# Tracing layer 0's products with values two key blocks behind their exponentials, for images 1 to 3

## The chip, the cores and the metric

The kernel runs on one core of one Trainium2 chip. The metric is the device time of one execution in microseconds; three executions before the change gave 4298.08, 4301.13 and 4314.65, median 4301.13. All arithmetic is in 32-bit floating point.

## The reference, cut to what matters

The input is a batch of 4 images of 32 x 32 positions with 384 channels. Four layers follow one another, each added to its input: deformable attention (layer 0), attention with a group weight (layer 1), a ratio of box sums (layer 2) and an outlook attention (layer 3). The change touches the attention of layer 0 alone:

```python
attn = jnp.einsum('bmhc,bnhc->bhmn', qh, k) * scale
...
bias = _bilinear_sample(rpe_img, disp)
bias = bias.reshape(Bq, G, n, n, GH).transpose(0, 1, 4, 2, 3).reshape(Bq, HEADS, n, n)
attn = jax.nn.softmax(attn + bias, axis=-1)
out = jnp.einsum('bhmn,bnhc->bmhc', attn, v).reshape(Bq, Hq, Wq, NC)
```

There are 6 heads of 64 channels and n = 1024 positions. Each head has 1024 x 1024 scores, and the bias is sampled bilinearly from a table at positions that depend on the key.

## The kernel before, in words

**Two lanes.** `Trunk` computes layers 1 to 3 of an image, `Front` computes layer 0. Image 0's layer 0 runs first, by itself and by a method of its own (`heads0`), which keeps a written-out order. After that, layer 0 of image b + 1 runs beside layers 1 to 3 of image b. Both lanes are Python generators that trace instructions. Each hands over by yielding a weight: a trunk image has weights that add up to 1109, a front image 714. `layer3` of the class `Net` (the driver) runs the trunk to its next yield, and then the front as long as it is less than a tenth of an image ahead. So weights decide only in which order the two lanes' instructions are traced. A half block of the trunk's attention (half of one key block j of a head pair in `pair`) has weight 7, which lets the front go on by about 4.5 of its units.

**From trace to queues.** The framework plans the order on each engine's queue from the trace: it steps through a model of the program and gives a free engine the ready instruction that was traced first. It also gives out buffers then. So the traced order is a priority, not the order of execution. Only `keep_in_program_order` and `issue_after` fix an order; the lines of `head0`, which the change touches, use neither. On the chip each engine works through its queue in order.

**A half head.** `head0(h, q)` does head h for half of the queries (q is 0 or 1, 512 queries). The 1024 keys are 8 blocks of 128 keys (NJ = 8); each block's scores are one tile `lg` of 128 keys x 512 queries. There are 12 half heads an image and 36 in the three images.

- For each key block a gather brings a window of the bias table (L955), ScalarE and VectorE interpolate it (L967 to L973), TensorE computes the products of keys and queries (L979), and VectorE adds (L982) and keeps a running maximum `rmax` (L984, L986). After every second block the front yields 6.
- The maximum over all keys is taken by transposes (L993), a reduction (L997) and a product that spreads it over the partitions (L1001). ScalarE copies it to `tb` (L1005). The front yields 3.
- For each key block VectorE subtracts `tb` (L1012), ScalarE takes the exponential in place (L1013), and TensorE adds the product with the values into one bank `po` (L1014). The values carry a column of ones, so `po` also holds the sum of the exponentials. After every second block the front yields 2.
- ScalarE copies the result out of `po` into `queries` (L1018) and the row of sums over the tile of the first block (L1027, in `sums_of`). SP issues the DMA of the sums to memory (L1020). The front yields 3.

After both halves of two heads, `over_sums` loads the sums back (L1283), inverts them and multiplies.

**Buffers.** The score tiles `lg` rotate through 13 buffers, of which a half head holds 8. The windows have 4. Accumulators of one bank come from `bank()`, with 4 buffers for both lanes: `po`, the scores' products (two at a time), the trunk's sums over keys `av` (L1690, held for a whole head pair), and the trunk's products of similarities (L1748) and transposes (L1743). Accumulators of two banks come from `big()`, with 2 buffers: the trunk's scores (L1718) and first pass (L1580).

**The trunk beside it.** For each key block of a head pair, `pair` traces scores (L1718), their exponentials (L1726) and four products (L1743, L1748). Each product's bank is read by VectorE (L1755) and, for some, copied by ScalarE (L1760). After the first two or three products it queues a step of the first pass for the next pair (L1580 on TensorE, L1589 on VectorE, L1593 on ScalarE).

Of the kernel before, what the change touches and what calls it, by code (L numbers as in the profile page):

```python
# [20 lines left out]
AF = mybir.ActivationFunctionType  # L21
ALU = mybir.AluOpType
# [8 lines left out]
NJ = N // P  # L31
# [35 lines left out]
def bc(ap, axis, n):  # L67

    u = ap.unsqueeze(axis)
    shape = list(u.shape)  # L70
    shape[axis] = n
    return u.broadcast_to(shape)
# [368 lines left out]
class Front(Lane):  # L441
# [500 lines left out]
    def head0(self, h, q):  # L942

        nc, v = self.nc, self.nc.vector
        f = self.f
        k, r0 = h // 2, (h % 2) * GC
        rows = slice(r0, r0 + GC)
        HH, HN = HW // 2, N // 2
        queries = self.qpad[rows, k, 1 + HH * q : 1 + HH * (q + 1), 1 : 1 + HW]
        logits = []  # L950
        rmax = self.wt([P, HN], "rmax", 2)
        for j in range(NJ):
            c = j * G + h
            win = self.wt([P, (HH + 1) * WROW], "win", 4)
            nc.gpsimd.indirect_dma_start(  # L955
                out=win,
                out_offset=None,
                in_=self.strips[:, :],
                in_offset=bass.IndirectOffsetOnAxis(
                    ap=self.widx[:, q, c : c + 1], axis=0  # L960
                ),
            )
            wv = win.rearrange("p (r c) -> p r c", c=WROW)
            sc = lambda i, t: f[:, i, t, c : c + 1]

            z = self.wt([P, HH, HW + 1], "z", 3)
            nc.scalar.activation(z, wv[:, 0:HH, 0 : HW + 1], AF.Copy, scale=sc(1, 1))  # L967
            v.scalar_tensor_tensor(  # L968
                z, wv[:, 1 : HH + 1, 0 : HW + 1], sc(0, 1), z, ALU.mult, ALU.add
            )  # L970
            lg = self.wt([P, HH, HW], "lg", 13)
            nc.scalar.activation(lg, z[:, :, 0:HW], AF.Copy, scale=sc(1, 0))  # L972
            v.scalar_tensor_tensor(lg, z[:, :, 1 : HW + 1], sc(0, 0), lg, ALU.mult, ALU.add)  # L973
            logits.append(lg.rearrange("p y x -> p (y x)"))
            if j % 2:
                ps = [self.bank() for _ in range(2)]
                for u in range(2):
                    w, mov = self.logits_of(h, q, j - 1 + u)
                    nc.tensor.matmul(ps[u], w, mov, start=True, stop=True)  # L979
                for u in range(2):  # L980
                    lf = logits[j - 1 + u]
                    v.tensor_tensor(lf, ps[u], lf, ALU.add)  # L982
                    if j - 1 + u == 1:
                        v.tensor_tensor(rmax, logits[0], lf, ALU.max)  # L984
                    elif j > 1:
                        v.tensor_tensor(rmax, rmax, lf, ALU.max)  # L986
                yield 6


        NI = HN // P  # L990
        ps = self.bank()
        for i in range(NI):
            nc.tensor.transpose(  # L993
                ps[:, i * P : (i + 1) * P], rmax[:, i * P : (i + 1) * P], self.ident
            )
        top = self.wt([P, NI], "top", 2)
        v.tensor_reduce(top, ps.rearrange("p (i n) -> p i n", i=NI), AX.X, ALU.max)  # L997
        diag = self.wt([P, NI, P], "diag", 1)
        v.tensor_tensor(diag, bc(self.ident, 1, NI), bc(top, 2, P), ALU.mult)
        ps = self.bank()  # L1000
        nc.tensor.matmul(  # L1001
            ps, self.ones, diag.rearrange("p i n -> p (i n)"), start=True, stop=True
        )
        tb = self.wt([P, HN], "tb", 2)
        nc.scalar.copy(tb, ps)  # L1005
        yield 3


        po = self.bank()
        for j in range(NJ):  # L1010
            lf = logits[j]
            v.tensor_tensor(lf, lf, tb, ALU.subtract)  # L1012
            nc.scalar.activation(lf, lf, AF.Exp)  # L1013
            nc.tensor.matmul(po, self.values_of(h, j), lf, start=j == 0, stop=j == NJ - 1)  # L1014
            if j % 2:
                yield 2

        nc.scalar.copy(queries, po[rows, :].rearrange("p (y x) -> p y x", y=HH))  # L1018
        den = self.sums_of(h, po, logits[0])
        nc.sync.dma_start(self.den[h][:, q * HN : (q + 1) * HN], den)  # L1020
        yield 3

    def sums_of(self, h, po, to):

# [1168 lines left out]
```

## Time and profile before

| | |
|---|---|
| median of three executions | 4301.13 us |
| the profiled execution | 4273.34 us |
| its span, first to last instruction | 4271.6 us |
| mean granted TensorE clock | 0.956 |
| TensorE busy | 3908.3 us, 91% |
| VectorE busy | 3109.2 us, 73% |
| ScalarE busy | 2300.2 us, 54% |
| GpSimd busy | 952.5 us, 22% |
| product with values (L1014), 576 instructions | 271.1 us busy, 17.2 us idle before |
| exponential (L1013), 288 instructions | 166.8 us busy, 29.5 us idle before |
| copy of the result (L1018), 36 instructions | waits 25.4 us for L1014, 11 times |

PE is TensorE, PEld its weight loads, DVE VectorE, ACT ScalarE, POOL GpSimd, SP the engine that issues most DMAs; a q after a name is the engine's sequencer. L1014 is line 1014 of the kernel before. A row such as "PE bank L1014 <- ACT lg L1013" tells that TensorE's instruction of L1014, which writes a tile named bank, waited for ScalarE's of L1013. One 32-bit product of 128 x 128 with 128 x 512 shows as two TensorE instructions. The profile's times come from one execution, which was 27.8 us shorter than the median.

### The profile page before, as it was taken

Reading aid. Unit: us, or ns where it says so; the run is one execution under the profiler, and the core shown is the slowest. Engines: PE = TensorE matmul, PEld = TensorE weight load, DVE = VectorE, ACT = ScalarE, POOL = GpSimd, SP = SyncE. Lnnn points to the kernel's source line nnn. Section 1 sums busy time; section 2 is a strip of 40 time slices with the busy share of each in tenths; the row PEclk is TensorE's granted clock in tenths of the full one; section 3 lists DMA queues with packets and bytes.
Section 4 is the critical chain, followed back from the end, with each engine's and each line's share of the span. In section 5 each row is a group of like instructions: output and inputs, shape, how many; then the busy total and the mean of one; then the engine's idle time right before and its main releaser. Section 6 shows DMA issues by size and latency. Waiting matters only on the chain.

```text
span 4271.6 us, 45276 instructions
## 1 busy us (share of the span) xinstructions
PE 3908.3 (91%) x14832; PEld 1680.1 (39%) x14832; DVE 3109.2 (73%) x5940; ACT 2300.2 (54%) x3640; POOL 952.5 (22%) x945
## 2 busy tenths in 40 slices
PE   8799989999999898999899989999999989999997
PEld 4333434333334443433333443433333434434443
DVE  4699676879888456787879837588888874566654
ACT  3277345667664333566767424376666542566633
POOL 1766152202121015221303002321121210000001
PEclk9899989999999998999999999999999999999998
DMA  7744353212221444321312163432221213210111
GB/s 162 227 133 124 88 162 100 72 43 83 61 82 41 143 137 145 104 71 47 96 39 84 33 195 123 137 97 61 60 84 51 79 63 120 86 39 23 34 34 45
DMA packets 295398, 385.09 MB, mean 90 GB/s; under 512 B 167858, under 2 KB 228798, under 8 KB 294650
## 3 DMA queue, kind: packets, MB, share of 16 engines
q1 hardware_dynamic: 246336, 217.44, 18.3%
q0 software_dynamic: 39936, 145.53, 11.6%
q10 hardware_dynamic: 8890, 19.23, 1.4%
q8 instruction: 118, 1.93, 0.2%
q14 instruction: 118, 0.97, 0.1%
HBM read 295.63 MB, written 86.75 MB: 90 GB/s over the span
## 4 chain that ended last, share of the span: by engine, by line
PE 52%; DVE 25%; ACT 8%; issue 6%; DMA 5%; POOL 3%; SPq 0%; DVEq 0%; ACTq 0%; POOLq 0%
PE bank L1748 12%; PE big L1718 6%; DVE nmax L1589 4%; PE big L418 4%; PE bank L1014 4%; PE big L1580 3%; PE bank L432 3%; DVE e L1755 3%; ACT big L1593 3%; PE bank L1690 3%; PE bank L1743 2%; PE bank L979 2%; POOL gat L762 2%; DVE lg L982 2%; PE big L678 2%
## 5 line engine op out<-in xcount | busy, mean ns | idle before, releaser
L1748 PE MATMUL bank<-whole,sg 128*128 128x512 f32 (+3 forms) x2304 | 844.8, 497 | 6.8 <-POOL sg L1701 5.3
L1755 DVE SCALAR_TENSOR_TENSOR e<-bank,gam,e 128x512 f32<-128x512 f32 x768 | 560.0, 746 | 273.5 <-PE bank L1748 179.9
L1593 ACT ACTIVATE big<-big,nmax 128x1024 f32<-128x1024 f32 x384 | 417.6, 1088 | 319.9 <-DVE nmax L1589 319.2
L1748 PEld LDWEIGHTS bank<-whole,sg 128*128 128x128 f32 x2304 | 397.0, 194 | 350.6 <-issue 258.1
L1589 DVE TENSOR_REDUCE nmax<-big 128x1 f32<-128x1024 f32 x384 | 451.9, 1217 | 57.3 <-PE big L1580 56.8
L955 POOL DMA_INDIRECT win<-strips,widx x288 | 310.9, 1080 | 781.2 <-DVE z L968 382.1
L1726 ACT ACTIVATE e<-big 128x1024 f32<-128x1024 f32 x384 | 380.2, 1020 | 188.1 <-PE big L1718 181.8
L1718 PE MATMUL big<-qa,ka 64*128 64x512 f32 x1536 | 423.4, 646 | 37.3 <-ACT big L1593 26.3
L1701 POOL TENSOR_SCALAR sg<-whole,gam 128x512 f32<-128x512 f32 x192 | 150.5, 784 | 1326.9 <-PE bank L1748 1009.0
L1580 PE MATMUL big<-k,q 32*128 32x512 f32 x1536 | 272.9, 670 | 51.7 <-ACT big L1593 30.2
L1014 PE MATMUL bank<-lg,va 128*128 128x512 f32 x576 | 271.1, 607 | 17.2 <-ACT lg L1013 17.1
L762 POOL DMA_INDIRECT gat<-pairs,sidx x192 | 220.3, 1148 | 293.1 <-DVE ix_one L561 235.8
L1718 PEld LDWEIGHTS big<-qa,ka 64*128 64x128 f32 x1536 | 145.7, 194 | 282.7 <-issue 110.8
L973 DVE SCALAR_TENSOR_TENSOR lg<-z,bias_f,lg 128x512 f32<-128x512 f32 x288 | 214.8, 762 | 36.6 <-ACT lg L972 35.3
L967 ACT ACTIVATE z<-win,bias_f 128x528 f32<-128x528 f32 x288 | 206.1, 736 | 52.9 <-DVE lg L973 31.9
L968 DVE SCALAR_TENSOR_TENSOR z<-win,bias_f,z 128x528 f32<-128x528 f32 x288 | 217.8, 767 | 21.8 <-ACT z L967 20.6
L1690 PE MATMUL bank<-e,vs 128*32 128x512 f32 x1536 | 221.5, 629 | 13.0 <-DVE vs L1684 13.0
L1012 DVE TENSOR_TENSOR lg<-lg,tb 128x512 f32<-128x512 f32 x288 | 184.1, 693 | 54.6 <-ACT tb L1005 54.6
L1760 ACT COPY gn<-bank 128x128 f32<-128x128 f32 (+2 forms) x288 | 106.3, 369 | 200.3 <-DVE e L1755 198.5
L972 ACT ACTIVATE lg<-z,bias_f 128x512 f32<-128x512 f32 x288 | 200.1, 716 | 10.0 <-DVE z L968 6.9
L982 DVE TENSOR_TENSOR lg<-bank,lg 128x512 f32<-128x512 f32 x288 | 190.7, 683 | 16.7 <-PE bank L979 16.2
L1013 ACT ACTIVATE lg<-lg 128x512 f32<-128x512 f32 x288 | 166.8, 624 | 29.5 <-DVE lg L1012 26.8
(331 smaller groups left out, 6338.1 us busy)
## 6 DMA issues: line engine op xcount, KB each, us to landing
q<-qd SPq DMA_DIRECT2D x48, 256.0 KB
xg<-xgd SPq DMA_DIRECT2D x48, 256.0 KB
pairs<-gat SPq DMA_DIRECT2D x48, 192.0 KB
w<-in_gmat SPq DMA_DIRECT2D x15, 576.0 KB
w<-in_Wqkv SPq DMA_DIRECT2D x12, 576.0 KB
a<-in_x SPq DMA_DIRECT2D x16, 384.0 KB
q<-qpad SPq DMA_DIRECT2D x12, 512.0 KB
qs<-q SPq DMA_DIRECT2D x24, 256.0 KB
```

The source lines that it names most:

```text
L762: pin(nc.gpsimd.indirect_dma_start(out=gat[:, g].rearrange("p l c -> p (l c)"), out_offset=None, in_=pairs[:, :], in_offset=bass.IndirectO ...
L955: nc.gpsimd.indirect_dma_start(out=win, out_offset=None, in_=self.strips[:, :], in_offset=bass.IndirectOffsetOnAxis(ap=self.widx[:, q, c : ...
L982: v.tensor_tensor(lf, ps[u], lf, ALU.add)
L1014: nc.tensor.matmul(po, self.values_of(h, j), lf, start=j == 0, stop=j == NJ - 1)
L1580: nc.tensor.matmul(ps[r][:, h * 512 : (h + 1) * 512], self.q4[rows, i * P : (i + 1) * P], self.k4[rows, 0:512], start=True, stop=True,)
L1589: top = v.tensor_reduce(nmax[:, r, i : i + 1], ps[r], AX.X, ALU.max, negate=True)
L1593: nc.scalar.activation(ps[r], ps[r], AF.Exp, bias=nmax[:, r, i : i + 1], accum_out=den[:, r, i : i + 1],)
L1690: nc.tensor.matmul(av[r0 : r0 + HD1, :], vs[:, r, :], es[h][:, r, :], start=j == 0, stop=j == NJ - 1,)
L1718: nc.tensor.matmul(ps[:, r, :], ka[rows, j * P : (j + 1) * P], qa[rows, cols], start=True, stop=True,)
L1726: nc.scalar.activation(e, ps, AF.Exp)
L1748: last = nc.tensor.matmul(ps[:, (mid - i0) * P :], sg[:, r, m, :], sim[:, h, r, m, (mid - i0) * P :], start=m == 0, stop=m == 1,)
L1755: v.scalar_tensor_tensor(e[:, r, :], ps, self.gam[:, 1:2], e[:, r, :], ALU.add, ALU.mult, accum_out=tot[:, r, h : h + 1],)
```

## The change

The loop over key blocks runs two steps longer. Step t traces the subtraction and the exponential of block t (for t under 8) and the product of block t - 2 (for t from 2). It yields 2 after every second step, so five times instead of four. The yield at the end of the half head is 1 instead of 3, and the weights still add up to 38 a half head. The arithmetic is the same, and so is the order of the additions into `po`. Images 1 to 3 use this method; image 0 does not.

```diff
         po = self.bank()
-        for j in range(NJ):
-            lf = logits[j]
-            v.tensor_tensor(lf, lf, tb, ALU.subtract)
-            nc.scalar.activation(lf, lf, AF.Exp)
-            nc.tensor.matmul(po, self.values_of(h, j), lf, start=j == 0, stop=j == NJ - 1)
-            if j % 2:
+        for t in range(NJ + 2):
+            if t < NJ:
+                lf = logits[t]
+                v.tensor_tensor(lf, lf, tb, ALU.subtract)
+                nc.scalar.activation(lf, lf, AF.Exp)
+            j = t - 2
+            if j >= 0:
+                nc.tensor.matmul(
+                    po, self.values_of(h, j), logits[j], start=j == 0, stop=j == NJ - 1
+                )
+            if t % 2:
                 yield 2
 
         nc.scalar.copy(queries, po[rows, :].rearrange("p (y x) -> p y x", y=HH))
         den = self.sums_of(h, po, logits[0])
         nc.sync.dma_start(self.den[h][:, q * HN : (q + 1) * HN], den)
-        yield 3
+        yield 1
```

## The prediction

> **What bounds the kernel now.** I read the page first (busy shares, chain), then busy time by stage, then TensorE's waits over the whole span, and last the timeline of single half heads.
>
> ```profile
> PE 3908.3 (91%) x14832; PEld 1680.1 (39%) x14832; DVE 3109.2 (73%) x5940; ACT 2300.2 (54%) x3640; POOL 952.5 (22%) x945
> ...
> PE 52%; DVE 25%; ACT 8%; issue 6%; DMA 5%; POOL 3%; SPq 0%; DVEq 0%; ACTq 0%; POOLq 0%
> ```
>
> TensorE is busy 91% of the span and holds half of the chain. The changed lines run only in three stretches, one an image, from 680 to 1410 us, 1725 to 2455 and 2770 to 3500, beside layers 1 and 2 of the image before. The first one, by stage (columns: length, then busy time of TensorE, weight loads, VectorE, ScalarE, GpSimd, then clock):
>
> ```profile
> 680.00:1300.00 620.00, 575.56 (x2301) 236.74 (x2302) 525.85 (x1046) 423.75 (x675) 136.26 (x138) 0.97 0.26 72
> 1300.00:1410.00 110.00, 101.48 (x300) 44.76 (x299) 89.37 (x145) 51.30 (x65) 10.14 (x8) 0.97 0.11 36
> ```
>
> There TensorE is idle 44.4 + 8.5 = 53 us of 730. The other two stretches give 46.3 + 8.5 and 43.3 + 8.5, together 160 us. The change removes no matmul, so those 160 us are all that it could win. TensorE's waits (total, times, longest) say how little belongs to the changed line:
>
> ```profile
> PE big L1580 <- ACT big L1593: 30.2, 11, 4.4
> PE big L1718 <- ACT big L1593: 26.3, 14, 2.6
> PE big L1580 <- ACT e L1726: 21.5, 36, 1.2
> PE bank L1014 <- ACT lg L1013: 17.1, 19, 2.4
> ...
> PE bank L1743 <- ACT lg L1027: 6.7, 6, 1.5
> ```
>
> L1014 is the product with values, L1013 its exponential: 17.1 us, 0.4% of the time. The first three lines are the trunk waiting for itself. The last is the trunk waiting for the bank that a half head's result leaves. One half head on TensorE (start, length, what):
>
> ```profile
> 758.75 1.12 PE L1001 MATMUL bank<-diag,ones 128*128 128x512 f32 x2
> 759.80 1.13 PE L1718 MATMUL big<-qa,ka 64*128 64x512 f32 x4
> 761.93 1.12 PE L1014 MATMUL bank<-lg,va 128*128 128x512 f32 x2 [1.01 <-ACT lg L1013]
> 762.90 1.02 PE L1748 MATMUL bank<-whole,sg 128*128 128x512 f32 x2
> 763.75 1.02 PE L1014 MATMUL bank<-lg,va 128*128 128x512 f32 x2
> 764.61 2.74 PE L1748 MATMUL bank<-whole,sg 128*128 128x512 f32 x6
> 767.28 1.14 PE L1580 MATMUL big<-k,q 32*128 32x512 f32 x8
> 768.35 5.42 PE L1014 MATMUL bank<-lg,va 128*128 128x512 f32 x12
> 773.61 3.60 PE L1748 MATMUL bank<-whole,sg 128*128 128x512 f32 x8
> ```
>
> One product is two instructions. The first waits 1.01 us for its exponential; the last six run in one batch, 4.5 to 6.3 us after their exponentials ended. The planner, which fills each queue by readiness and takes the order of the trace as a priority, thus already keeps the distance that the change writes down. Going through all 36 half heads in the timeline in this way, idle time stands only before first products or a few early ones. In each image it is 1.0 us in half heads 1 and 3, 0.46 in 10, 0.50 in 11 and 2.41 in 12, and half head 9 has 0.15, 0.92 and 0: 3 x 5.37 + 1.07 = 17.2 us. In the other six half heads the products lag by 1.9 us or more and wait for nothing.
>
> **The change part by part.** Counting the weights of the hand-overs gives the order of the trace; it is the same for all three images. A trunk step of 7 pays for 7/1109 x 714 = 4.5 front units, and the new order puts each pair of products 2 units later, so about 0.44 trunk half blocks go ahead of it.
>
> *Added and removed instructions: none.* 8 subtractions, 8 exponentials, 8 products, 2 copies and one DMA issue a half head stay. The weights still add up to 11 (8 + 3 before, 10 + 1 after), so all else keeps its place. Cost 0; the added hand-over itself executes nothing.
>
> *First pair of products.* It moves behind one trunk half block in half heads 1, 3, 10 and 11 of each image. In half head 1 the products of L1748 that follow it started without a wait, so they can fill the pause: 2 x 1.0 + 0.46 + 0.50 = 2.96 us an image, **-8.9 us**. In half heads 9 and 12 no trunk step lies in between (8.3 us stay); in 12 ScalarE has an activation-table load of 1.28 us in front of the first exponential, which no order on TensorE hides. The ends are 0 and the whole -17.2.
>
> *Later pairs.* They have nothing to gain from their own exponentials. As later work they can fill pauses of the trunk: L1580 waits 36 times for L1726, 21.5 us in all. Those after this half head (0.62 at 782.70 and 1.03 at 784.85) lie 8 to 10 us behind the end of the last pair's present place, and a move past one half block is 3.60 us (the row at 773.61), so most stay out of reach. I take two pauses of 0.6 us an image, 3.6, rounded to **-3 us**; the ends are 0 and -21.5. Their score tiles come free later too: of the 13, 5 are spare, and ScalarE's L972 waits for a product 3 times, 2.1 us in all. The next half head's scores fill that tile by tile over 40 us, so I take 0; if that cover is gone, the 3.60 us land on the front, which runs a tenth of an image ahead.
>
> *Result bank and copies.* Half heads 2, 4, 5, 7 and 10 trace the two copies (L1018, L1027) behind one more trunk half block; in 1, 3, 6, 8 and 9 the last pair moves behind one while its copies stay. The bank is one of four; the trunk's sums over keys (L1690) hold a second for a whole pair. So L1743 and L1748 share two while it is open. On ScalarE the copies are queued ahead of scores (L972) and the trunk's copies (L1760) and exponentials (L1726). L1018 waits 11 times for its product now, 25.4 us, while ScalarE is 68% busy in the stage. The price is the row L1743 <- L1027, 1.1 us each: today 6 of 36 half heads pay it. If of the 12 new late ones (4 an image, as half head 2 pays already) one in six pays, it is +2; if all pay, +13. If the planner opens the bank later as well and today's waits vanish, -6.7. I take **+5**, nearer to +2, since two more banks let most half heads pass today.
>
> The Trainium skill, Perfetto Trace Analysis, under Optimization Strategy, holds that the same gap repeating on the engine that should be saturated can mean a lack of tiles or PSUM. The waits on L1027 do repeat in each image; taken at its word for all 30 half heads that close late, 33 us would stand for the +5, and the sum would be +21.
>
> *SP's queue.* The issue of the sums (L1020) waits for L1027, and what is traced behind it on SP waits along:
>
> ```profile
> SPq L1020 <- ACT lg L1027: 884.6, 36, 53.2
> ```
>
> At 777.40 the issue goes out, and the next one comes at 811.79: 34 us of cover in odd half heads. In even ones, division loads (840.68) and the trunk's next queries and keys (844.16) follow at once; they would start later by the copy's delay, at most 3.60 us, and are used a pair later. I take 0; without cover it would be 18 x 3.60 = 65 us, an end that nothing in the waits of TensorE points to. GpSimd's gathers are traced at the same distances as before.
>
> **Sum:** -8.9 - 3 + 5 = -7 us. The profiled execution took 4273.34 us (span 4271.6 and 1.7 around it), so it would become 4266. It is 27.8 us under the median of the runs; on the median, 4301 - 7 = **4294 us**. A measurement of this kernel can tell about 0.5% from no change, 21.5 us.
>
> **The rivals.**
>
> *The order has no effect where it counts.* The planner keeps the hardware order, since its clock already delays the products; for this speak the lags of 1.9 us and more, against it the priority that flips at one to three trunk steps a half head. Time: 4301.
>
> *The result bank closes late (slower).* The last pair or the copies fall behind a trunk half block in 30 of 36 half heads, and the products that need the bank stall one after another. With one stall of 1.1 us in each: 33 - 6.7 already paid - 8.9 = +17, 4318; with two, 66 - 15.6 = +50, 4351; the middle is 4335. It ends over 0.5% slower from (21.5 + 15.6) / 30 = 1.24 us a half head. For it: two working banks, and 25.4 us of ScalarE waiting at the copy. Against it: the bank also opens later in 12 half heads.
>
> *The pairs become fillers (faster).* If all 21.5 us of L1580 <- L1726 are filled, beside -8.9: -30, 4271. For it: trunk first is the better priority where TensorE is 93% busy. Against it: where those pauses lie.
>
> **How the numbers follow.** Forecast 0.46 (own range 4277 to 4308: from -24, both gains larger with the bank at no cost, to +7); no effect 0.11; bank closes late 0.27; fillers 0.16. Of the fillers some 0.14 and of the forecast 0.06 end over 0.5% faster: 0.20. Of the late bank 0.21 and of the forecast 0.06 end over 0.5% slower: 0.27. The rest, 0.53, lies within. The range runs from the fillers' 4271 to a little over the late bank's middle, 4338, and leaves out about one in ten at either side.
>
> **What would show it.** In the profile after: L1014 <- L1013 falls from 17.1 to some 8 us, with the 2.41 left at half head 12; first products start 4 to 6 us after the exponentials in half heads 1 and 3; L1743 <- L1027 stays under 15 us; TensorE's busy time stays at 3908. Wrong it would be if L1743, L1748 or L1718 gained a wait of over 20 us in the three stretches, if the copies L1018 made ScalarE wait far over 25.4 us, or if pauses of the trunk outside these lines moved: then the planner laid the queues differently for reasons that this trace does not show.

## The result and the profile after

The changed kernel takes 4330.4 us, the kernel before 4304.4 us on the same chip (medians of eight runs each). The ratio is 1.0069, with a 95% interval of 1.0051 to 1.0087. By this ratio the change makes the kernel slower by about 30 us, or 22 to 37 us by the interval; the two medians lie 26 us apart. The prediction was 4294 us, a gain of 7 us on 4301.

The page after has the same 14832 TensorE instructions as before, but they are busy 25 us longer (3908.3 before):

```profile
PE 3933.4 (91%) x14832; PEld 1677.6 (39%) x14832; DVE 3107.3 (72%) x5940; ACT 2303.3 (53%) x3640; POOL 954.0 (22%) x945
```

Up to the first changed half head, near 760 us, the two programs have the same order on TensorE, VectorE, ScalarE and GpSimd. Yet the profiled execution after is already 16.3 us late there (its first copy of the row maxima starts at 776.25, before at 759.91), and TensorE has been busy for 675.4 us instead of 663.3. So 12 of the 25 us have nothing to do with the change, and I don't compare the whole spans of the two profiles, but only the lengths of half heads. A half head is measured from the copy of its row maxima (`tb`, L1005) to that of the next one. Lines after the loop lie 5 lower in the changed kernel, and in the loop the line numbers differ: the product with values is now L1017, its exponential L1014, the trunk's transposes L1748, its similarities L1753, its exponential L1731 and VectorE's read of the bank L1760.

These are TensorE's waits in the changed kernel (total us, times, longest). Before, the transposes' wait for VectorE's read was not among the rows, and the other four had 17.1, 1.4, 3.4 and 6.7 us:

```profile
PE bank L1748 <- DVE e L1760: 13.2, 6, 3.5
...
PE bank L1017 <- ACT lg L1014: 10.0, 9, 2.4
...
PE bank L979 <- DVE lg L982: 8.0, 6, 1.9
...
PE bank L979 <- DVE e L1760: 5.5, 3, 1.9
...
PE bank L1748 <- ACT lg L1032: 4.6, 3, 1.5
```

The product's own wait fell as intended. New are waits for a bank that VectorE has to empty first. The wait that the prediction watched, the last row (L1743 <- L1027 before), fell from 6.7 to 4.6 us.

By half head, after minus before, in us for images 1, 2 and 3 (columns of experiments are explained below; the same order mostly varies by up to 1.8 us between executions, through the clock, and in single places by more: +4.2 us in half head 6 of image 3 in run 6):

| half head | after | last pair late in 6, 8, 9 | bank held in 6, 9 |
|---|---|---|---|
| 1 | -1.4, -1.2, -1.5 | 0, 0, 0 | 0, 0, 0 |
| 3 | -1.1, -1.1, -1.1 | 0, 0, 0 | 0, 0, 0 |
| 6 | +3.6, +2.1, +2.2 | +4.3, -0.3, +4.5 | +4.1, +2.9, +4.4 |
| 8 | +2.6, +4.6, +3.8 | +3.2, +4.2, +4.0 | -1.3, +0.4, -0.5 |
| 9 | +3.8, +1.6, +2.2 | +1.5, +1.0, +2.3 | +0.9, +0.3, +0.9 |

Half heads 6, 8 and 9 lose 26.5 us in the three images together, 1 and 3 gain 7.4. What the loss looks like shows best in half head 6. This is its end on TensorE before (start, length, instruction, and in brackets the idle time ahead and what ended it):

```profile
1068.08 3.70 PE L1014 MATMUL bank<-lg,va 128*128 128x512 f32 x8
1071.71 1.99 PE L1718 MATMUL big<-qa,ka 64*128 64x512 f32 x8
1073.62 1.09 PE L1743 MATMUL bank<-ident,gf 128*128 128x128 f32 x8
1076.23 0.33 PE L1743 MATMUL bank<-ident,gn 128*128 128x128 f32 x1 [1.51 <-ACT lg L1027]
1076.39 1.46 PE L1748 MATMUL bank<-whole,sg 128*128 128x384 f32 x4
```

And this is the same place in the changed kernel:

```profile
1081.80 3.70 PE L1017 MATMUL bank<-lg,va 128*128 128x512 f32 x8
1085.43 1.99 PE L1723 MATMUL big<-qa,ka 64*128 64x512 f32 x8
1087.34 1.09 PE L1748 MATMUL bank<-ident,gf 128*128 128x128 f32 x8
1088.28 1.02 PE L1017 MATMUL bank<-lg,va 128*128 128x512 f32 x2
1092.84 0.48 PE L1748 MATMUL bank<-ident,gn 128*128 128x128 f32 x1 [3.54 <-DVE e L1760]
1093.11 2.77 PE L1753 MATMUL bank<-whole,sg 128*128 128x384 f32 x4
1095.81 2.09 PE L1585 MATMUL big<-k,q 32*128 32x512 f32 x8
1097.83 1.47 PE L1017 MATMUL bank<-lg,va 128*128 128x512 f32 x2
```

Before, the last product ends at 1071.7, ScalarE copies the result out, and the trunk's transposes of `gn` take the bank that this frees, after 1.51 us. After, the last product stands behind the trunk's half block, at 1097.83. The result's bank is still open when the transposes want one, so they wait for another bank, the one that VectorE's L1760 empties. L1760 needs an exponential of the trunk, which ScalarE starts at 1089.68, after scores of the next half head, and VectorE starts L1760 at 1092.03. The pause is 3.54 us in all three images. Behind it the rows are nearly twice as long: L1753's four took 2.77 us where they took 1.46 before. The windows of that place show why (bounds, length, busy time and count of TensorE, weight loads, VectorE, ScalarE and GpSimd, then the granted clock):

```profile
1080.00:1088.00 8.00, 8.00 (x33) 2.98 (x32) 6.90 (x12) 7.19 (x14) 1.71 (x2) 1.00 0.06 17
1088.00:1093.00 5.00, 1.46 (x8) 0.63 (x6) 4.43 (x9) 4.83 (x7) 3.72 (x4) 0.87 0.52 163
1093.00:1096.00 3.00, 3.00 (x9) 1.32 (x13) 1.20 (x4) 0.74 (x1) 0.41 (x1) 0.50 0.71 206
1096.00:1099.00 3.00, 3.00 (x10) 0.82 (x10) 2.36 (x4) 0.37 (x1) 0.94 (x1) 0.57 0.02 7
```

The clock is 0.50 behind the pause. Half head 6 of image 1 is 3.6 us longer with the same 236 instructions, and only 1.0 us of this is idle time (6.2 to 7.2 us); 2.6 us are slower rows, which count as busy time. Three such pauses make 10.6 of the 13.2 us in the first row of waits above.

Half head 9 has a shorter pause of the same kind (1.13 us in L979, waiting for a bank that ScalarE's copy of `gn` empties).

In half head 8 it is something else. Its idle time went from 9.3 to 7.8 us in image 1, from 7.9 to 8.3 in image 2 and from 8.3 to 9.2 in image 3, and its clock is no lower than before. What grew is the time that TensorE is busy. The scores of two key blocks are two products of two instructions each, on 64 partitions each, into two banks. Before, they start in pairs, and the four instructions take 1.1 us:

```profile
1201.44 0.69 PE L979 MATMUL bank<-qpad,kz 64*128 64x512 f32 x1
1201.45 0.69 PE L979 MATMUL bank<-qs,kz 64*128 64x512 f32 x1
1201.97 0.59 PE L979 MATMUL bank<-qpad,kz 64*128 64x512 f32 x1
1201.98 0.59 PE L979 MATMUL bank<-qs,kz 64*128 64x512 f32 x1
```

In the changed kernel one product runs behind the other, and they take 2.1 us (the last two rows):

```profile
1211.14 1.12 PE L979 MATMUL bank<-qpad,kz 64*128 64x512 f32 x2
1212.92 0.69 PE L979 MATMUL bank<-qs,kz 64*128 64x512 f32 x1 [0.66 <-ACT lg L1032]
...
1222.58 1.12 PE L979 MATMUL bank<-qpad,kz 64*128 64x512 f32 x2
1223.55 1.12 PE L979 MATMUL bank<-qs,kz 64*128 64x512 f32 x2
```

All rows of L979 in half head 8 of image 1, before and after (bounds, length, TensorE's time in these rows and their count, granted clock, DMA share and GB/s):

```profile
1169.30:1233.16 63.86, 6.09 (x16) 0.95 0.28 82
1188.38:1254.86 66.48, 9.27 (x16) 0.97 0.22 67
```

In images 2 and 3 it is 5.4 us before and 8.8 and 8.4 after. The trunk's products of 32 partitions (L1637, now L1642) grow from 2.3 to 2.8 us to 4.5 us in the same way, and one score product of the trunk, 1 us, has moved here from half head 9. Runs 2 and 5, which have a late last pair here, show it too (L979 8.4 to 8.8 us). That the open bank separates the two products is likely, since each needs a bank of its own, but here only the first pair shows it: its second product, at 1212.92, waits 0.66 us for the copy (L1032) that empties the result's bank.

Half heads 1 to 11 of the three images together are 26.0 us longer, 13 us of it idle and 13 us busy, while the clock is at 0.50 for less time (92 us instead of 106). So a lower clock explains half head 6, not the sum.

### The profile page after: what moved, and what is told of

The parts are those of the page before. It is cut to its first block, busy times and chain, and to the rows that moved or that the text cites. A ratio compares the mean times of both kernels' runs of the same rounds, so it can differ in the third digit from the quotient of the medians.

```text
span 4328.9 us, 45276 instructions
## 1 busy us (share of the span) xinstructions
PE 3933.4 (91%) x14832; PEld 1677.6 (39%) x14832; DVE 3107.3 (72%) x5940; ACT 2303.3 (53%) x3640; POOL 954.0 (22%) x945
## 4 chain that ended last, share of the span: by engine, by line
PE 52%; DVE 27%; ACT 9%; issue 7%; DMA 4%; POOL 2%; SPq 1%; another core or an unknown queue 0%; ACTq 0%; DVEq 0%; POOLq 0%
PE bank L1753 11%; PE big L1723 6%; DVE nmax L1594 4%; PE big L1585 4%; PE big L418 4%; PE bank L1017 3%; PE bank L432 3%; DVE e L1760 3%; ACT big L1598 3%; PE bank L1748 2%; PE bank L1695 2%; DVE lg L982 2%; DVE lg L973 2%; PE bank L979 2%; DVE z L968 1%
## 5 line engine op out<-in xcount | busy, mean ns | idle before, releaser
L1753 PE MATMUL bank<-whole,sg 128*128 128x512 f32 (+3 forms) x2304 | 841.9, 496 | 1.8 <-POOL sg L1706 0.3
L1760 DVE SCALAR_TENSOR_TENSOR e<-bank,gam,e 128x512 f32<-128x512 f32 x768 | 561.3, 747 | 280.4 <-PE bank L1753 181.4
L1753 PEld LDWEIGHTS bank<-whole,sg 128*128 128x128 f32 x2304 | 394.6, 193 | 344.2 <-issue 267.9
L1731 ACT ACTIVATE e<-big 128x1024 f32<-128x1024 f32 x384 | 379.7, 1019 | 201.8 <-PE big L1723 195.6
L1723 PE MATMUL big<-qa,ka 64*128 64x512 f32 x1536 | 434.1, 647 | 39.9 <-ACT big L1598 24.1
L1017 PE MATMUL bank<-lg,va 128*128 128x512 f32 x576 | 275.8, 613 | 10.4 <-ACT lg L1014 10.0
L762 POOL DMA_INDIRECT gat<-pairs,sidx x192 | 210.7, 1097 | 326.8 <-DVE ix_one L561 237.0
L1013 DVE TENSOR_TENSOR lg<-lg,tb 128x512 f32<-128x512 f32 x288 | 185.9, 694 | 52.8 <-ACT tb L1005 52.8
L972 ACT ACTIVATE lg<-z,bias_f 128x512 f32<-128x512 f32 x288 | 200.0, 717 | 31.7 <-DVE z L968 25.8
L979 PE MATMUL bank<-qs,kz 64*128 64x512 f32 x288 | 166.5, 661 | 22.3 <-DVE lg L982 8.0
```

The source lines that it names most:

```text
L1017: nc.tensor.matmul(po, self.values_of(h, j), logits[j], start=j == 0, stop=j == NJ - 1)
L1723: nc.tensor.matmul(ps[:, r, :], ka[rows, j * P : (j + 1) * P], qa[rows, cols], start=True, stop=True,)
L1731: nc.scalar.activation(e, ps, AF.Exp)
L1753: last = nc.tensor.matmul(ps[:, (mid - i0) * P :], sg[:, r, m, :], sim[:, h, r, m, (mid - i0) * P :], start=m == 0, stop=m == 1,)
L1760: v.scalar_tensor_tensor(e[:, r, :], ps, self.gam[:, 1:2], e[:, r, :], ALU.add, ALU.mult, accum_out=tot[:, r, h : h + 1],)
```

## The experiments

All are edits of the kernel before. In them `weigh(j)` stands for the subtraction and exponential of block j and `product(j)` for its product with values. The kernel before took 4272 us on the chip of the first four runs, 4274 us on that of the next four, and 4303 us on that of the last three, so ratios are compared, not times. In the expectations, LAST PAIR names the theory that the late last pair keeps the result's bank open, COPIES that the later copies on ScalarE cost, and LAG that the distance between exponentials and products costs by itself.

**1. The lag, with the last pair where it was.** The first three pairs are traced one hand-over late, the last one in its old place ahead of the copies.

```diff
-        for j in range(NJ):
+        for step in [
+            [("e", 0), ("e", 1)],
+            [("e", 2), ("m", 0), ("e", 3), ("m", 1)],
+            [("e", 4), ("m", 2), ("e", 5), ("m", 3)],
+            [("e", 6), ("m", 4), ("e", 7), ("m", 5), ("m", 6), ("m", 7)],
+        ]:
+            for what, j in step:
+                (weigh if what == "e" else product)(j)
+            yield 2
...
         yield 3
```

> The lag of two blocks stays for the first three pairs of products, the last pair is traced where it was before, and the added hand-over is undone (2, 2, 2, 2, 3). Theory LAST PAIR (the last pair of products, put behind a trunk half block, keeps the result bank open in half heads 6, 8 and 9): those losses of some 9 us an image are gone and the 2.5 to 3.5 us an image gained in half heads 1 to 3 stay, so 5 to 12 us under the kernel before. Theory COPIES (the added hand-over puts the two copies out of the bank behind trunk work): also without the loss, 0 to 10 us under before. Theory LAG (products later than their exponentials are themselves the loss): as the changed kernel, 20 to 30 us over before.

Measured: ratio 0.9990 (0.9977 to 1.0004), 4 us under before, where LAST PAIR asked for 5 to 12 and COPIES for 0 to 10. Over all half heads the lag costs nothing, so LAG falls. But this is a sum: run 11, with the same order in half heads 1 and 3 alone, is 24 us under before, so the lag costs some 20 us in the others (run 9 finds a part of it).

**2. The last pair late, the rest as before.**

```diff
+        for step in [
...
+            [("e", 4), ("m", 4), ("e", 5), ("m", 5)],
+            [("e", 6), ("e", 7)],
+            [("m", 6), ("m", 7)],
+        ]:
...
-        yield 3
+        yield 1
```

> Only the last pair of products is traced one hand-over later, with the copies behind it as in the changed kernel; the other three pairs are traced as before. LAST PAIR: 25 to 35 us over the kernel before, since the losses of half heads 6, 8 and 9 are there and the gain of the first pair is not. COPIES: 20 to 30 us over. LAG: a quarter of the changed kernel's loss, 5 to 8 us over.

Measured: ratio 1.0063 (1.0047 to 1.0079), 27 us and nearly the whole loss of 1.0069 by this part alone. LAST PAIR asked for this, but so did COPIES, since the copies come behind the pair.

**3. Only the added hand-over ahead of the copies.**

```diff
+        for step in [
...
+            [("e", 6), ("m", 6), ("e", 7), ("m", 7)],
+            [],
+        ]:
...
-        yield 3
+        yield 1
```

> All products are traced as before; only the added hand-over is there, so that the two copies and the issue of the sums come one hand-over later. LAST PAIR: within 5 us of the kernel before. COPIES: 20 to 30 us over. LAG: 0.

Measured: ratio 1.0002 (0.9990 to 1.0014). But the run tells less than it should. In its profile the copies ran at the same distance from the row maxima as before (half head 6: the bank closes 19.2 us after them before, and so here): they were traced later and put back to where they were ready. So it says that the added hand-over costs nothing, not what late copies would cost. Run 7 does that.

**4. The whole change in heads 0 and 1 alone.**

```diff
+        lag = 2 if h < 2 else 0
-        for j in range(NJ):
+        for t in range(NJ + lag):
...
-        yield 3
+        yield 3 - lag
```

> The whole change for heads 0 and 1 (half heads 1 to 4 of each image), the order of before for heads 2 to 5. LAST PAIR: no half head that loses is changed, 7 to 12 us under the kernel before. COPIES: half heads 2 and 4 have their copies behind a trunk half block, 4 of the 10 of an image that close later, so 5 to 12 us over. LAG: a third of the changed kernel's loss, 7 to 10 us over.

Measured: ratio 0.9959 (0.9944 to 0.9973). The same change is a gain of 17 us in half heads 1 to 4, more than the 7 to 12 of LAST PAIR, and a loss in the others. COPIES and LAG, which asked for a loss here, fall. The last pair falls behind a trunk half block in half heads 1 and 3 too; there the early part of the change gives more than the late pair takes. (In run 2, which has the late pair without the rest, half head 1 was 0.5, 1.6 and 1.6 us longer and half head 3 0.9 us in each image.)

**5. The last pair late in half heads 6, 8 and 9 alone.** From the profile, these are where the loss shows.

```diff
+        behind = (h, q) in ((2, 1), (3, 1), (4, 0))
         for j in range(NJ):
             weigh(j)
-            product(j)
+            if not (behind and j >= NJ - 2):
+                product(j)
             if j % 2:
                 yield 2
+        if behind:
+            product(NJ - 2)
+            product(NJ - 1)
+            yield 2
...
-        yield 3
+        yield 1 if behind else 3
```

> The order of before, but in half heads 6, 8 and 9 of each image (head 2's and head 3's second, head 4's first) the last pair of products is traced one hand-over later and the copies behind it. BANK (the loss comes from these three half heads, because the result's bank stays open behind a half block of the trunk): the stretches of half heads 6, 8 and 9 grow by 6 to 10 us an image together, ratio to before 1.004 to 1.007, that is most of the changed kernel's 1.0069. SPREAD (the loss is spread over the half heads whose products or copies come later, and these three only show it most): ratio 1.000 to 1.003.

Measured: ratio 1.0091 (1.0077 to 1.0104), more than BANK expected and more than the whole change. Three places an image hold the loss. Their stretches are longer by 24.7 us in the profiled execution, where the ratio stands for 39 us (33 to 44), so 8 us or more are not located. In image 3 much of the 4.5 us of half head 6 is chance: the clock stayed at 1.00 behind its pause of 3.79 us, and only at its end came 13.65 us at 0.50, as in run 6 at the same place, with the order of before.

**6. The whole change except in half heads 6, 8 and 9.**

```diff
+        lag = 0 if (h, q) in ((2, 1), (3, 1), (4, 0)) else 2
```

> The whole change, but half heads 6, 8 and 9 of each image have the order of before. BANK: the loss is gone and the gain of half heads 1 to 4 stays, ratio 0.995 to 0.999. SPREAD: more than half of the loss stays, ratio 1.003 to 1.006.

Measured: ratio 0.9997 (0.9986 to 1.0008). The loss is gone, so SPREAD falls. But the gain of run 4 did not show either, just outside what BANK had: something in the other half heads eats it (run 9).

**7. The bank held open, all products in place.** In half heads 6 and 9 the two copies are queued on ScalarE behind a later exponential of the trunk. The products with values keep their places.

```diff
+                if j == 1 and self.late:
+                    with self.tc.issue_after(SEEN[0]):
+                        self.late()
+                    self.late = None
...
+        def close():
+            nc.scalar.copy(queries, po[rows, :].rearrange("p (y x) -> p y x", y=HH))
+            den = self.sums_of(h, po, logits[0])
+            nc.sync.dma_start(self.den[h][:, q * HN : (q + 1) * HN], den)
+
+        if (h, q) in ((2, 1), (4, 0)):
+            self.late = close
+        else:
+            close()
...
-                nc.scalar.activation(e, ps, AF.Exp)
+                SEEN[:] = [nc.scalar.activation(e, ps, AF.Exp).ins]
```

The first lines stand in the next half head, behind its first hand-over; `SEEN` holds the trunk's latest exponential.

> All products stay where they are in before, TensorE's order is that of before. Only in half heads 6 and 9 of each image are the two copies that empty the result's bank queued behind a later exponential of the trunk, so the bank is held open some 10 to 15 us longer. BANK (what costs is that one of the four banks is held, whoever holds it): half heads 6 and 9 grow by 2 to 4 us each, ratio 1.002 to 1.006. PLACE (what costs is the last pair's later place in TensorE's order, not the bank): these half heads stay within 1 us, ratio 0.9985 to 1.0015.

Measured: ratio 1.0036 (1.0023 to 1.0048). Half head 6 grew by 4.1, 2.9 and 4.4 us, as BANK said, half head 9 by only 0.9, 0.3 and 0.9, within the 1 us of PLACE. The bank of half head 6 closes 36.5 us after the row maxima instead of 19.2. This is its TensorE; the lines are 24 lower than before (L1767 transposes, L1772 similarities, L1779 VectorE's read):

```profile
1074.51 1.09 PE L1767 MATMUL bank<-ident,gf 128*128 128x128 f32 x8
1075.54 1.05 PE L1714 MATMUL bank<-e,vs 128*32 128x512 f32 x2
1080.80 0.47 PE L1767 MATMUL bank<-ident,gn 128*128 128x128 f32 x1 [4.21 <-DVE e L1779]
1081.06 2.70 PE L1772 MATMUL bank<-whole,sg 128*128 128x384 f32 x4
```

The products had ended at 1072.6, 14.8 us after the row maxima as before, and still the same transposes wait for VectorE and the next rows are slow. So a held bank costs without a late product. TensorE's order is not quite that of before, though the expectation had it so: two of the trunk's sums over keys (L1714) come ahead of the transposes. And the run also moves the two copies on ScalarE, but the row that waits is for a bank. In half head 9 the held bank accounts for a half or less of the loss of run 5. There the scores' products no longer all start in pairs: their rows (L984) take 5.8 to 5.9 us instead of 5.0, with the clock at 1.00, which is its growth in images 1 and 3.

**8. A larger dose: the last pair two trunk half blocks late in half heads 6 and 9.**

```diff
+                if j == 1 and self.late:
+                    self.late()
+                    self.late = None
...
+        behind = (h, q) in ((2, 1), (4, 0))
+        for j in range(NJ):
+            weigh(j)
+            if not (behind and j >= NJ - 2):
+                product(j)
...
+        def close():
+            if behind:
+                product(NJ - 2)
+                product(NJ - 1)
```

> The order of before, but in half heads 6 and 9 of each image the last pair of products and the copies are traced behind the next half head's first scores, two half blocks of the trunk later where the changed kernel has one. BANK: the loss grows with the time that the bank is open; half heads 6 and 9 with the stretch behind each cost 8 to 16 us an image together, ratio 1.005 to 1.011. PLACE (a late pair costs the same however late it is): 4 to 6 us an image together as in the changed kernel, ratio 1.002 to 1.004.

Measured: ratio 1.0054 (1.0040 to 1.0069). The two half heads grew by 8.8, 3.7 and 5.8 us together. This lies between the two expectations and doesn't tell them apart. Beside the others it says one thing: in half head 6 of image 1 the bank was open 17.8 us in run 5, 31.7 in run 7 and 32.9 here (14.4 before), and the half head grew by 4.3, 4.1 and 7.1 us. The cost is not in proportion to the time. This suggests that most of it falls due once the one request for a bank that this one used to serve finds it open; with the clock's chances of up to 4 us it is not shown.

**9. The whole change in half heads 10, 11 and 12 alone.**

```diff
+        lag = 2 if (h, q) in ((4, 1), (5, 0), (5, 1)) else 0
```

> The whole change in half heads 10, 11 and 12 of each image alone (head 4's second half and head 5), the rest as before. What is asked is where the gain of heads 0 and 1 goes when the rest of the change is made too. TAIL (the products two blocks late cost time at the end of the heads, where the result of half head 12 closes later and the next stage waits for it): 1 to 5 us an image longer, ratio 1.001 to 1.004. WAITS (as the prediction had it, the waits of 0.46 and 0.50 us of half heads 10 and 11 fall away and nothing else): ratio 0.999 to 1.0005.

Measured: ratio 1.0021 (1.0007 to 1.0035), a loss of 9 us, as TAIL said. Two of TensorE's waits answer to it (L1767 is VectorE's read here; before they had 3.4, 3 times, at most 1.1, and 1.0, 3 times, at most 0.4):

```profile
PE bank L1017 <- ACT lg L1014: 16.2, 16, 2.4
...
PE bank L979 <- DVE e L1767: 5.9, 4, 1.9
PE big L418 <- DVE qpad L1309: 4.8, 3, 1.6
```

Half head 10 loses its product's wait of 0.46 us, and its scores (L979) wait 0.7 us longer for a bank instead. Half head 11 keeps its 0.50. In half head 12 of image 1 the bank closes 20.0 us after the row maxima instead of 17.4, and the projection that needs all six heads (L418) waits 1.2 us longer. Run 1, whose last pair is in its old place, has these two rows as well (5.3 us in L418, 5.5 in L979), so this part of the cost belongs to the lag.

**10. The whole change in half heads 1 and 3 alone.**

```diff
+        lag = 2 if h < 2 and q == 0 else 0
```

> The whole change in half heads 1 and 3 of each image alone (first halves of heads 0 and 1), the rest as before: the two places whose first pair waits 1.0 us in before. FIRST PAIR (the gain of heads 0 and 1 comes from these two first pairs, each with the stretch of lowered clock behind its wait): the two half heads 1.0 to 1.6 us shorter each, ratio 0.995 to 0.998. ONLY THE WAITS (they are worth the 1.0 us each that the rows show, 6 us in all, and the rest of the gain of heads 0 and 1 came from elsewhere): ratio 0.998 to 0.9995.

Measured: ratio 0.9966 (0.9953 to 0.9979), a gain of 15 us (9 to 20), as FIRST PAIR had it. The stretches of these two half heads are 1.4 to 1.5 and 1.1 us shorter, 7.7 us in all, so part of the gain lies where the profile doesn't show it. The run can't tell that the lowered clock gave it: in images 2 and 3 half head 1 still had 3.4 us of lowered clock and was as much shorter.

**11. The same two, with the last pair kept in place.**

```diff
+        lag = 2 if h < 2 and q == 0 else 0
+        for t in range(NJ):
+            weigh(t)
+            if t >= lag:
+                product(t - lag)
+            if t == NJ - 1 and lag:
+                product(NJ - 2)
+                product(NJ - 1)
...
         yield 3
```

> As the run with half heads 1 and 3 alone, but their last pair of products stays where it is in before, with the copies, so the result's bank is open some 5 us instead of 3 us less than in before. BANK AS IN HALF HEAD 6 (an earlier close helps wherever the half head lies): 0.5 us or more a half head better than that run, ratio lower by 0.0007 or more. BANKS SPARE HERE (in heads 0 and 1 no instruction waits for the bank, so its time is free): the same ratio within 0.0007, 0.995 to 0.998.

Measured: ratio 0.9942 (0.9925 to 0.9958), 24 us faster than before and the best of all. Half head 1 is 1.9 to 2.1 us shorter, 0.4 to 0.6 more than in run 10; half head 3 is the same. The ratio is 0.0024 lower than that of run 10, but the intervals overlap by 0.0005. The ratio and half head 1 speak for BANK AS IN HALF HEAD 6, as do half heads 1 and 3 of run 2. Half head 3, whose bank closes 3.0 us earlier than in run 10 without a gain, speaks for BANKS SPARE HERE. It is not settled. Its row of the product:

```profile
PE bank L1017 <- ACT lg L1014: 10.1, 12, 2.4
```

What is left of it are the half heads 9 to 12, where the order is that of before.

**The sum.** The parts run alone give -0.34% (half heads 1 and 3), +0.91% (6, 8 and 9) and +0.21% (10 to 12), together +0.78%; the whole change has +0.69% (0.51 to 0.87). Without the middle term it would be -0.13%, and run 6 has -0.03% (-0.14 to +0.08). The account closes within the intervals.

## Why the prediction was wrong

**The step that failed is "Result bank and copies".** It took +5 us, from "if of the 12 new late ones (4 an image, as half head 2 pays already) one in six pays, it is +2", and "nearer to +2, since two more banks let most half heads pass today". Run 5 measures 39 us in place of the 5, by three half heads an image; and the whole change loses some 31 us against run 6, which leaves these three as they were. Three things in the step were wrong:

- *Where.* The step counted mainly the half heads whose copies move. Run 3 shows that the added hand-over moves no copy and costs nothing. Of the five whose last pair moves, which the step named as well, 1 and 3 lose 0.5 to 1.6 us by it (run 2), and 6, 8 and 9 nearly all the rest. That the other banks let most half heads pass is a statement on an average. In half heads 6, 8 and 9 it failed, and the trace of before said so in one line: the transposes of half head 6 already waited 1.51 us for this very bank.
- *The price.* The 1.1 us of L1743 <- L1027 is what it costs to wait for a bank that is about to be freed. When it stays open for another half block, as in half head 6, the transposes no longer wait for it: they wait for another bank, and the row has another name. So L1743 <- L1027 fell, under the 15 us that the prediction had as its sign, while the loss stood under VectorE's L1760 and the like. The sign that should have shown the step wrong, one wait of over 20 us on the trunk's lines, did not come either; the largest new one there has 13.2.
- *More than the pause.* A pause was priced at its length. In half head 6, 1.0 us of more idle time came with 2.6 us of slower rows. In half head 8 the scores' products took 3 us more because they ran one behind the other, a cost that no row of waits shows.

**The rival "the result bank closes late" was right**, in mechanism and nearly in size: 4335 us against 4330.4. But its sum was one or two stalls of 1.1 us in 30 half heads; it was three half heads an image with 1.6 to 4.6 us each. So the nearness of the figure is luck. The prediction spoke against it with "the bank also opens later in 12 half heads". It does, by 3.6 us in half heads 1 and 3, but not in 6 and 8, where the first product starts 4.8 us after the row maxima in both kernels, and in 9 it opens 0.1 to 0.2 us later in two images and 0.9 us earlier in one.

**The Trainium skill's rule was nearer than the step.** Perfetto Trace Analysis, under Optimization Strategy, takes a gap that repeats on the engine that should be saturated as a possible lack of PSUM; the prediction put +21 us for the sum by it. Run 7 agrees: to hold one bank longer, with the products with values in their places, cost 0.36%.

**"First pair of products" was right for half heads 1 and 3**: 1.0 us each was predicted, 1.1 to 1.5 measured in the stretches, with no wait left there. The first products start 3.7 us behind their exponentials, where 4 to 6 were expected. Run 10 gains more than these stretches show, 15 us, and where the rest lies is open. The part was wrong for 10 and 11. The 0.46 us of half head 10 went, but a later wait for a bank took its place, and the 0.50 of half head 11 stayed; together with 12 this part is +9 us, not -3 (run 9). The row L1014 <- L1013 fell to 10.0 us where "some 8" was expected, and half head 12 has 2.8 of it instead of 2.41.

**"Later pairs"** had -3 us from pauses of L1580 <- L1726. That row fell from 21.5 to 17.4 us, but run 1, with the lag and no late bank, is no faster than before, so there is no sign that it paid; its own share is not measured. **SP's queue** at 0 is not tested: in run 3, made with the hand-over ahead of the issue, the copies that the issue waits for did not move.

## What to carry to other kernels

Count an accumulator's bank from its first product to the copy that empties it, and ask at each place who takes that bank next; a product that may come late without anybody waiting for it still holds the bank. Where two products into two banks run side by side, as the scores here, they need both banks free at the same time. If a reordering moves several places at once, price each place by its own rows and try them apart: here the same edit gains 0.34% in two half heads an image (run 10) and loses some 0.7% in three (the whole change against run 6). Move the first product behind its exponential where it waits, keep the last one early (run 11), and leave the other half heads alone: the same order in all of them gains nothing (run 1).

## What the runs showed of the hardware

A pause on TensorE often cost more than itself. The two pauses for a bank shown above (3.54 and 4.21 us) came with a granted clock of 0.50 for 6.8 and 3.4 us, from 1.1 and 0.7 us before their end, and the rows behind them took 2.77 and 2.70 us instead of 1.46. The Trainium skill, TensorE: Matmul & The Clock Gate, Part 1, has it that an idle window of some 3.4 us halves the clock; these two agree. At this place the changed kernel and runs 2, 5 and 7 have twelve such pauses, of 3.5 to 4.3 us; ten came with the lower clock and two did not, as this one in image 3 of run 5, with the window behind it:

```profile
3183.08 0.33 PE L1758 MATMUL bank<-ident,gn 128*128 128x128 f32 x1 [3.79 <-DVE e L1770]
```

```profile
3183.10:3190.00 6.90, 6.28 (x30) 2.24 (x30) 6.39 (x11) 5.14 (x9) 3.26 (x4) 1.00 0.74 199
```

And the kernel before shows the lowered clock after much less. Its half head 1, TensorE and then one window:

```profile
782.70 1.12 PE L1580 MATMUL big<-k,q 32*128 32x512 f32 x2 [0.62 <-ACT e L1726]
784.85 1.56 PE L1580 MATMUL big<-k,q 32*128 32x512 f32 x6 [1.03 <-ACT e L1726]
```

```profile
784.00:788.00 4.00, 3.15 (x10) 0.81 (x10) 3.95 (x9) 3.34 (x6) 2.66 (x3) 0.68 0.66 206
```

Two pauses of 0.62 and 1.03 us within 2.2 us, and the clock is at 0.50 from 785.43 to 788.84, 3.4 us. On the other hand the single pause of 1.01 us at 761.93 was not followed by it. What sum of pauses in what time sets it off can't be read from these runs, and such windows also make the same order differ from one execution to the next, mostly by up to 1.8 us a half head and once by 4.2 us.
